# Smaller pieces for the first two images' inverse transforms, biases folded into the key and value weights, and a re-planned list schedule

## The chip, the cores and the metric

The kernel runs on one core of one Trainium2 chip. The metric is the device time of one execution in microseconds (us). Three runs of the kernel before gave 6176.5, 6177.5 and 6183.15 us; the median, 6177.5 us, is the time that counts. Engine names are those of the profile: PE is the matrix engine, PEld its weight loads, DVE the vector engine, ACT the scalar engine, POOL the GpSimd engine, SP the queue that starts most DMAs. A name with a q behind it (ACTq, PEq) is that engine's instruction queue when it issues or waits and computes nothing.

## The reference, cut to what matters

32 images of 128 channels and 64 x 64 pixels in float32 pass through two layers:

```python
x = x + conv(group_norm(x))            # butterfly transforms along w and h, a channel mix
                                       # per frequency, two inverse transforms, real part
t = to_tokens(x)                       # 4096 tokens of 128 channels for each image
n = layer_norm(t)
k = n @ Wk.T + bk                      # one 128 x 128 score matrix for each image:
v = n @ Wv.T + bv                      # its softmax replaces the sequence attention
t = t + n @ softmax(k.T @ v / sqrt(32)).T
n = layer_norm(t)
t = t + top2_gated_sum(n @ expert_w + expert_b, softmax(n @ router_w + router_b))   # 8 experts
x = from_tokens(t)
```

All eight experts are computed for each token, and the gates are zero for six of them.

## The kernel before, in words

The work has three stages, one after the other. **Stage 1** (to about 930 us) norms each image and takes it through the two forward transforms into `xf` in DRAM. **Stage 2** (to about 2550 us) goes through the 64 columns of frequencies: it builds the weights of a column (L610), mixes the channels of all images with them (L632) and stores the result to `pf` in DRAM (L651), eight stores for each half of the output channels. **Stage 3** (the rest) goes through the 32 images, one in about 109 us.

In stage 3 an image `b` passes through three functions, a slot apart, so that three images are in work at once:

- `conv(b)`: eight tiles `r0` to `r7` (two DMAs of 256 KB each, L825) come from `pf` by SP. `w_inverse(e)` (L838) multiplies one into a tile `pu` of two PSUM banks; there is a single such tile (pool `cps`, tag `cv`). `w_out` (L848) copies it to `u` on ACT, in four copies of 64 partitions by 512 elements. Then `h_inverse(g)` (L860) makes `py` from `u`, in the same two banks, and `h_out` (L868, DVE) adds it to the image `y` (one DMA of 2 MB, L819).
- `front(b)`: transposes to tokens (`pt` L919, copied by ACT L924), their moments on DVE (L893 to L906), a power on POOL (L911), normed tokens `xg` on ACT (L959), and their product with themselves `pg` (L970). `xg` has 129 columns, of which the last is one, so that `pg` also holds the sum over the tokens. From `pg` comes a chain of small steps on PE, DVE and ACT in turn: `gsum` (L983), `rows_mm` (`pa`: L987, L988, L989), `rows_out` (L994), `kv1` (`pb`: L998, L999), `kv1_out` (L1003), `kv2` (L1007, L1008), softmax (L1012 to L1027), `attn` (`pc`: L1031, L1032). L989, L999 and L1008 are products with one row, and bring in the two biases. Then `product` (`pp` L1058), `scaled` on ACT (L1071, L1075), `added` on DVE (L1086), second moments and gates.
- `experts(b)`: normed tokens (`xn` L1186), turned (`px` L1196, `xT` L1202), 64 products with the experts' weights (`pe` L1209, 128 x 512 each, three buffers of one bank, pool `eps`), each gated by DVE (`tm` L1220), summed by POOL (L1245, L1246, L1248), turned back (`po` L1255) and stored (L1261). In the last image DVE sums some pairs itself (L1232).

Every float32 product stands in the trace as two matmul records; a transpose is one.

The order on each engine is worked out when the kernel is built. `add(b, key, engine, us, at, run, after, take, free)` gives an operation its engine, an assumed duration `us`, a due time `at` in slots (moved by `SHIFT` for its kind of key), what it follows, and which buffers it takes and frees. `Plan.run` then plays the engines through with these durations: a free engine starts the earliest due operation whose predecessors and buffers are there. The order so found is issued as it is, and each engine works through its queue in that order, so that an operation that has to wait holds up what is queued behind it on its engine.

Ahead of the stage 3 plan stand its constants (L736 to L792): weights and biases by ACT's queue (L738 to L767), memsets on POOL (L753 to L762, L779), and a preparation that takes the experts' weights' mean out and adds their bias (`pm` L783, L784, L788; `pms` L791, L792). These are outside of the ordered block, and the trace shows them placed between its first instructions.

Of the kernel before, what the change touches and what calls it, by code (L numbers as in the profile page):

```python
# [90 lines left out]
def kernel(  # L91
# [57 lines left out]
    gmean = gmean.rearrange("p g r -> p (g r)")  # L149
    mhalf = cp.tile([P, NT], F32, name="mhalf")  # L150
# [7 lines left out]
    with ExitStack() as ph1:  # L158
# [274 lines left out]

        def butterfly(m, engine, eng, at, us):
# [76 lines left out]
        for s in range(B + 2):  # L511
# [23 lines left out]
            if s == 6:  # L535
                add("wr", "PE", 0.6, 6.0, weight_rows, [("b0", 5), "sel"], ("ps",))
                add("wd", "DVE", 0.8, 6.0, weight_matrices, ["wr"], (), ("ps",))
                butterfly(2, "POOL", nc.gpsimd, 7.0, 4.5)
                add("wo", "DVE", 1.2, 9.0, output_matrices, [("b2", 5)])
                add("wm", "SP", 0.5, 10.0, weight_taps, [("b2", 5)], (), (), 4.0)  # L540
            if 12 <= s < 16:
# [184 lines left out]

    cps = ctx.enter_context(tc.tile_pool(name="cps", bufs=1, space=PSUM))
    eps = ctx.enter_context(tc.tile_pool(name="eps", bufs=3, space=PSUM))
    tps = ctx.enter_context(tc.tile_pool(name="tps", bufs=3, space=PSUM))
    xp = ctx.enter_context(tc.tile_pool(name="xp", bufs=2))  # L730
    rp = ctx.enter_context(tc.tile_pool(name="rp", bufs=10))
# [5 lines left out]
    wk_sb = ct.tile([P, P], F32, name="wk_sb")  # L737
    nc.scalar.dma_start(wk_sb, wkT)  # L738
    wv_sb = ct.tile([P, P], F32, name="wv_sb")
    nc.scalar.dma_start(wv_sb, wvT)  # L740
    bk_sb = ct.tile([1, P], F32, name="bk_sb")
    nc.scalar.dma_start(bk_sb, bk.unsqueeze(0))
    bv_sb = ct.tile([1, P], F32, name="bv_sb")
    nc.scalar.dma_start(bv_sb, bv.unsqueeze(0))
    rb_sb = ct.tile([P, NE], F32, name="rb_sb")
    nc.scalar.dma_start(rb_sb, router_b.partition_broadcast(P))
    ew_sb = ct.tile([P, NE, P], F32, name="ew_sb")
    nc.scalar.dma_start(ew_sb, expert_w.rearrange("e d c -> d e c"))
# [5 lines left out]
    ntok = ct.tile([1, 1], F32, name="ntok")  # L754
    nc.gpsimd.memset(ntok, float(NPIX))
    ones = ct.tile([P, P], F32, name="ones")
    nc.gpsimd.memset(ones, 1.0)

    NG = 4
    xg = [ct.tile([P, 4, P + 1], F32, name=f"xg{i}") for i in range(NG)]  # L760
    for t in xg:
        nc.gpsimd.memset(t[:, :, P : P + 1], 1.0)  # L762
# [9 lines left out]
    with tc.tile_pool(name="prep", bufs=1) as prep:  # L772

        ebb = prep.tile([P, NE, P], F32, name="ebb")
        nc.scalar.dma_start(
            ebb.rearrange("p e c -> p (e c)"), expert_b.rearrange("e c -> (e c)").partition_broadcast(P)
        )
        om = prep.tile([P, P], F32, name="om")
        nc.gpsimd.memset(om, 1.0 / P)  # L779
# [9 lines left out]

        pe = eps.tile([P, 512], F32, tag="pe", name="pms")  # L790
        nc.tensor.matmul(pe[:, 0:NE], ones, prx[0][:, P + NE : QX], start=True, stop=True)  # L791
        nc.vector.tensor_copy(rws, pe[:, 0:NE])  # L792
# [5 lines left out]
        "ad": 0.75, "at": -0.21, "f": 0.63, "gt": 0.63, "h": -0.15, "ho": -1.5, "l": 0.63, "lg": 0.15,  # L798
        "m": -0.08, "na": -0.08, "pe": 0.49, "pg": -0.45, "pt": -0.03, "pwa": -0.08, "pwb": 0.15,
        "r": -0.33, "s": 0.1, "sa": 0.33, "so": -0.09, "st": 0.47, "to": 0.52, "va": -0.08, "vb": 0.15,  # L800
        "wo": 0.12, "x": 0.44, "xT": 0.44, "xg": 0.12, "xn": 0.35,
# [12 lines left out]
    xs, rs, tile_of = {}, {}, {}  # L814

    def transfers(b):
# [4 lines left out]
        def load_r(e):  # L821
            def run():
                t = rs[b, e] = rp.tile([P, 16 * n], F32, tag="r", name=f"r{b}_{e}")
                for r in range(2):
                    nc.sync.dma_start(t[r * n : (r + 1) * n], pfv[b, e, r])  # L825
            return run

        for e in range(8):
            add(b, f"r{e}", "SP", 0.2, b - 0.5 + 0.08 * e, load_r(e), take=("r",), late=5.0)
        add(b, "x", "SP", 0.1, b + 0.2, load_x, take=("x",), late=12.0)  # L830

    def conv(b):
# [39 lines left out]

        for e in range(8):
            at = b + 0.08 * e
            add(b, f"w{e}", "PE", 1.8, at, w_inverse(e), [f"r{e}"] + [(b - 1, f"h{k}") for k in range(4)], ("cv",), ("r",))
# [5 lines left out]
        for g in range(4):  # L881
            at = b + 0.68 + 0.07 * g
            add(b, f"h{g}", "PE", 2.15, at, h_inverse(g), [f"wo{e}_{oh}" for e in range(8) for oh in range(2)], ("cv",))
            add(b, f"ho{g}", "DVE", 1.25, at, h_out(g), [f"h{g}", "x"], (), ("cv",))

    def front(b):
# [8 lines left out]
        def moments(which):  # L895
# [3 lines left out]
            m2 = st.tile([P, 5, NT], F32, name=f"m2{which}_{b}", tag=f"m2{which}", bufs=2)  # L899
            total, diff, var, nmr, rstd = (m2[:, k, :] for k in range(5))  # L900
# [37 lines left out]
        for g in range(8):  # L938
            at = s1 + 0.016 * g
            add(b, f"pt{g}", "PE", 0.55, at, turn(g), [(b - 2, f"st{g}")] + [f"ho{k}" for k in range(4)], ("tl",))  # L940
# [5 lines left out]
        def nmr1():  # L946
            total, var, nmr, rstd = v[1]
            nc.vector.scalar_tensor_tensor(nmr, total, -0.5, rstd, ALU.mult, ALU.mult)

        add(b, "na", "DVE", 0.9, s1 + 0.14, nmr1, ["pwa"])  # L950

        def norm(g):
            def run():
                total, var, nmr, rstd = v[1]
                for k in range(4):
                    i = 4 * g + k
                    nc.scalar.activation(  # L959
                        xg[g % NG][:, k, 0:P], t[:, i, :], AF.Identity, bias=nmr[:, i : i + 1], scale=rstd[:, i : i + 1]  # L960
# [3 lines left out]
        def gram(g):  # L964
            def run():
                if g == 0:
                    v["pg"] = tps.tile([P, 512], F32, tag="tl", name=f"pg{b}")
                for k in range(4):
                    i = 4 * g + k
                    nc.tensor.matmul(  # L970
                        v["pg"][:, 0 : P + 1], xg[g % NG][:, k, 0:P], xg[g % NG][:, k, :],
# [4 lines left out]
        for g in range(8):  # L976
            at = s1 + 0.26 + 0.016 * g
            add(b, f"xg{g}", "ACT", 1.7, at, norm(g), ["na", (b if g >= NG else b - 1, f"pg{(g - NG) % 8}")], ("xg",))
            add(b, f"pg{g}", "PE", 1.06, at, gram(g), [f"xg{g}"] + ([f"pg{g - 1}"] if g else []), ("tl",) if g == 0 else (), ("xg",))
# [375 lines left out]
```

## Time and profile before

| | |
|---|---|
| median of three runs | 6177.5 us |
| the profiled execution's own time | 6179.07 us |
| its span, first to last instruction | 6177.3 us |
| stage 1, stage 2, stage 3 | about 930, 1620, 3625 us |
| from one image's L983 to the next, images 3 to 30 | 109.05 us |
| busy over the span: PE, POOL, DVE, ACT | 97%, 68%, 68%, 61% |
| granted PE clock, mean | 0.99 |

The page divides the span into 40 slices of 154 us and gives the busy share of each engine in tenths. Other views give the busy time in a stretch, a timeline by engine, who waited for whom, and all instructions of one line. A row of the timeline has the start, the time from the first start to the last end of a run of like instructions, the engine, the line, the tiles written and read, their shape and their number; behind it, in brackets, stands idle time before it and what ended that. PE's instructions overlap, so that what one costs in a full queue is the distance from its start to the next start, and not its duration.

### The profile page before, as it was taken

To read this page: it belongs to the slowest core of one execution; us is meant where nothing else is said; L and a number is where in the kernel's file an instruction comes from. 1 tells how busy PE (TensorE), PEld (TensorE's weight loads), DVE (VectorE), ACT (ScalarE), POOL (GpSimd) and SP (SyncE) were. 2 spreads that over 40 slices of the span, in tenths; PEclk is the share of its full clock that TensorE was granted. 3 is DMA by queue.
4 is the path that set the end of the run, shared out by engine and by line. 5 is a ranking of instruction groups with operands and counts; after the bars stand their busy time and mean duration, and the time that the engine had idled before them with its cause. 6 is when DMAs were issued, how large, how long until landed. Compare 5 with 4: busy or idle time off the path is not lost. (4 is left out here: it accounts for less than half of the span.)

```text
span 6177.3 us, 218388 instructions
## 1 busy us (share of the span) xinstructions
PE 5988.3 (97%) x94922; PEld 4714.0 (76%) x94922; DVE 4213.0 (68%) x7686; ACT 3759.2 (61%) x7089; POOL 4187.1 (68%) x3755
## 2 busy tenths in 40 slices
PE   7999999999999999789999999999999999999988
PEld 7999998999999999666666666666666666666654
DVE  5565545555555555358778787787878778787777
ACT  7666654555555555376666666766667666666753
POOL 2110006666666666238888888888888888888888
PEclk9999999999999999899999999999999999999999
DMA  6766666666666666622222222222212222131100
GB/s 201 236 227 232 233 213 170 173 172 171 174 172 172 172 172 172 160 74 95 69 84 78 65 96 64 88 76 71 91 62 94 67 86 78 64 96 64 67 21 26
DMA packets 556965, 756.55 MB, mean 122 GB/s; under 512 B 58466, under 2 KB 321892, under 8 KB 551908
## 3 DMA queue, kind: packets, MB, share of 16 engines
q1 hardware_dynamic: 554096, 741.38, 39.9%
q8 instruction: 745, 12.21, 0.9%
q14 instruction: 216, 1.77, 0.1%
q10 hardware_dynamic: 1908, 1.19, 0.1%
HBM read 406.80 MB, written 335.54 MB: 120 GB/s over the span
## 5 line engine op out<-in xcount | busy, mean ns | idle before, releaser
L1209 PE MATMUL pe<-ew_sb,xT 128*128 128x512 f32 x4096 | 1984.6, 601 | 44.8 <-DVE tm L1220 40.6
L1220 DVE TENSOR_TENSOR tm<-pe,oh 128x512 f32<-128x512 f32 x2028 | 1341.2, 684 | 535.0 <-PE pe L1209 422.4
L1245 POOL TENSOR_TENSOR tm<-tm 128x512 f32<-128x512 f32 x1014 | 1296.3, 1293 | 314.6 <-DVE tm L1220 263.4
L1209 PEld LDWEIGHTS pe<-ew_sb,xT 128*128 128x128 f32 x4096 | 691.0, 191 | 518.7 <-issue 333.1
L621 DVE COPY f<-g 128x1024 f32<-128x1024 f32 x512 | 627.2, 1225 | 665.7 <-PE g L610 665.7
L632 PE MATMUL m<-f,s 128*64 128x64 f32 x32768 | 1071.3, 224 | 5.0 <-POOL s L583 3.6
L632 PEld LDWEIGHTS m<-f,s 128*64 128x64 f32 x32768 | 1000.7, 138 | 66.8 <-POOL s L583 3.9
L583 POOL COPY s<-l 128x512 f32<-128x512 f32 x512 | 546.5, 1102 | 599.2 <-issue 518.7
L621 ACT COPY f<-g 128x1024 f32<-128x1024 f32 x512 | 518.5, 1013 | 576.9 <-PE g L610 550.3
L1248 POOL TENSOR_TENSOR tk<-tk,tm 128x256 f32<-128x256 f32 x1014 | 753.4, 743 | 79.5
L848 ACT COPY u<-pu 64x512 f32<-64x512 f32 x1024 | 594.1, 580 | 308.3 <-PE pu L838 285.0
L1246 POOL TENSOR_TENSOR tm<-tm 128x512 f32<-128x512 f32 x507 | 647.0, 1276 | 39.8
L838 PEld LDWEIGHTS pu<-qw,r 128*128 128x128 f32 x4096 | 503.6, 196 | 170.1 <-ACT u L848 92.2
L610 PE MATMUL g<-c,wst 9*128 9x128 f32 x16384 | 609.2, 284 | 4.6 <-ACT f L621 3.4
L838 PE MATMUL pu<-qw,r 128*128 128x128 f32 x4096 | 522.6, 282 | 63.3 <-ACT u L848 52.9
L610 PEld LDWEIGHTS g<-c,wst 9*128 9x128 f32 x16384 | 510.9, 187 | 40.6 <-ACT f L621 4.5
L344 POOL TENSOR_TENSOR grstd<-gms,mhalf 128x1 f32<-128x1 f32 x32 | 17.8, 555 | 735.6 <-DVE gms L340 735.6
L585 POOL TENSOR_SCALAR s<-l 128x512 f32<-128x512 f32 x256 | 509.5, 1990 | 0.0
L413 PE MATMUL pf<-ph,v 128*128 128x128 f32 x4096 | 491.4, 278 | 5.2 <-ACT z L378 1.1
L1261 ACT COPY so<-po 128x512 f32<-128x512 f32 x256 | 150.9, 590 | 563.0 <-issue 411.9
L893 DVE BATCH_NORM_STATS2 bs<-tk 128x6 f32<-128x128 f32 x2048 | 448.2, 279 | 56.3 <-ACT tk L924 44.2
L413 PEld LDWEIGHTS pf<-ph,v 128*128 128x128 f32 x4096 | 467.1, 192 | 15.1 <-ACT z L378 7.1
(166 smaller groups left out, 8499.9 us busy)
## 6 DMA issues: line engine op xcount, KB each, us to landing
xf<-f SPq DMA_DIRECT2D x512, 256.0 KB, 3.3
l<-xf SPq DMA_DIRECT2D x1024, 128.0 KB, 3.3
pf<-o SPq DMA_DIRECT2D x1024, 128.0 KB, 3.3
r<-pf SPq DMA_DIRECT2D x512, 256.0 KB, 4.8
x<-in_x_dram SPq DMA_DIRECT2D x256, 256.0 KB, 4.6
y<-in_x_dram SPq DMA_DIRECT2D x32, 2048.0 KB, 8.1
out_dram<-so SPq DMA_DIRECT2D x256, 256.0 KB, 2.1
tw<-in_tw_dram SPq DMA_DIRECT2D x6, 384.0 KB, 6.6
```

The source lines that it names most:

```text
L413: nc.tensor.matmul(pl[:, j * P : (j + 1) * P], vs[b][:, 8 * g + j, :], ph.rearrange("h r m -> h (r m)"), start=True, stop=True,)
L583: nc.gpsimd.tensor_copy(dst, src)
L610: nc.tensor.matmul(pg[g // 2][:, g % 2, m * P : (m + 1) * P], wst[rows, 16 * half + 4 * t + m, :], c[rows].rearrange("r h k -> r (h k)"), ...
L621: copy(f.rearrange("i m (g o) -> i m g o", g=2), tile_of["g", w, half, t][k].rearrange("i g (o m) -> i m g o", o=4))
L632: nc.tensor.matmul(ps[hh * n : (hh + 1) * n, q, :], s[:, h].rearrange("i k b -> i (k b)")[:, B * r : B * r + n], f[:, h, r, :], start=(r = ...
L838: nc.tensor.matmul(ps[:, k, :], rs[b, e][:, k * P : (k + 1) * P], qw.rearrange("w r m -> w (r m)"), start=True, stop=True,)
L848: nc.scalar.copy(u[r * n : (r + 1) * n, :, oh * n + 8 * e : oh * n + 8 * e + 8], ps[oh * n : (oh + 1) * n, :, r * n : (r + 1) * n].rearran ...
L1209: nc.tensor.matmul(ps, tile_of["xT", b, i // 4][:, i % 4, :], ew_sb[:, es, :].rearrange("d e c -> d (e c)"), start=True, stop=True,)
L1220: nc.vector.tensor_tensor(tile_of["tm", b, i // 2][:, i % 2, es, :], tile_of.pop(("pe", b, i, half)).rearrange("p (e c) -> p e c", c=P), t ...
L1245: nc.gpsimd.tensor_tensor(tm[:, k, 0:4, :], tm[:, k, 0:4, :], tm[:, k, 4:8, :], ALU.add)
L1246: nc.gpsimd.tensor_tensor(tm[:, :, 0:2, :], tm[:, :, 0:2, :], tm[:, :, 2:4, :], ALU.add)
L1248: nc.gpsimd.tensor_tensor(t[:, lo : lo + 2, :], t[:, lo : lo + 2, :], tm[:, :, m, :], ALU.add)
```

## The change

- **Biases in the weights.** `wk_sb`, `wv_sb`, `bk_sb`, `bv_sb` become one tile `wkv`. In the preparation the mean over the input channels is taken out of both weight matrices and a 128th of the bias added to every row (`pmk`, two DVE operations, as the experts' weights already had it). The first norm of `front` now gives the normed tokens plus one (bias `nmr + 1`, a new row `above`), and its row sum, 128 for each token, then brings the bias in. `xg` and `pg` have 128 columns. `rows_mm`, `rows_out` and the two row products of `kv1` and `kv2` are gone.
- **First two images.** For `b < 2` each `w_inverse` is split in two pieces of one bank, `w{e}_0` and `w{e}_1`, each of 32 smaller matmuls (two logical 64 x 64 results for each of 8 k), which use the three `pe` buffers. A piece is copied by one ACT copy of 128 partitions by 512 elements. `h_inverse` and `h_out` are split in two likewise. Other images are as before.
- **Loads.** The loads of `r0` and `r1` of image 0 are issued by POOL's queue and those of `r2` and `r3` by ACT's; they run ahead of the plan, behind the preparation. The other loads stay on SP.
- **Preparation.** `ew_sb`, `ebb` and `om` become constants that stage 1 loads on SP in four steps, in its slots 20 to 23. The preparation is moved into the ordered block, as its first part. `pms` uses `om` and a factor of 128 in place of a matrix of ones.
- **Order of pools.** `rp` (the tiles `r`) is opened before `xp`, so that it gets other memory, and `eps` before `cps`.
- **The schedule.** Assumed durations are changed (`w` 1.8 to 1.9, `h` 2.15 to 2.05, `pt`, `px`, `st` 0.55 to 0.48, `pg` 1.06 to 0.9, `pp` 0.3 m to 0.26 m, `pb` and `pb2` 0.7 to 0.35), and so is the table `SHIFT`. The order on all engines of stage 3 comes out of these anew.

```diff
+        def expert_load(k):
+            def run():
+                es = slice(2 * k, 2 * k + 2)
+                nc.sync.dma_start(ew_sb[:, es, :], expert_w[es].rearrange("e d c -> d e c"))
+                nc.sync.dma_start(
+                    ebb[:, es, :].rearrange("p e c -> p (e c)"), expert_b[es].rearrange("e c -> (e c)").partition_broadcast(P)
+                )
+            return run
...
+            if 20 <= s < 24:
+                add(("ew", s), "SP", 1.0, s, expert_load(s - 20), [("pf", s - 3, 4)], (), (), 4.0)
...
+    def prepare():
...
+        pe = eps.tile([P, 512], F32, tag="pe", name="pmk")
+        nc.tensor.matmul(pe[:, 0 : 2 * P], om, wkv.rearrange("d e c -> d (e c)"), start=True, stop=True)
+        nc.vector.scalar_tensor_tensor(
+            kvb.rearrange("p e c -> p (e c)"), kvb.rearrange("p e c -> p (e c)"), 1.0 / P, pe[:, 0 : 2 * P],
+            ALU.mult, ALU.subtract,
+        )
+        nc.vector.tensor_add(wkv, wkv, kvb)
...
-            return run
+                    queue.dma_start(t[r * n : (r + 1) * n], pfv[b, e, r])
+            return run
+
+        if b == 0:
+
+            first.extend(load_r(e, nc.gpsimd if e < 2 else nc.scalar) for e in range(4))
...
+        def w_inverse_piece(e, oh):
+
+            def run():
+                ps = tile_of["cw", b, e, oh] = eps.tile([P, 8, n], F32, tag="pe", name=f"pw{b}_{e}_{oh}")
+                for k in range(8):
+                    lo = (2 * k + oh) * n
+                    for r in range(2):
+                        nc.tensor.matmul(
+                            ps[r * n : (r + 1) * n, k, :], rs[b, e][:, lo : lo + n], qw[:, r, :], start=True, stop=True
+                        )
+            return run
+
+        def w_out_piece(e, oh):
+            def run():
+                nc.scalar.copy(
+                    u[:, :, oh * n + 8 * e : oh * n + 8 * e + 8],
+                    tile_of.pop(("cw", b, e, oh)).rearrange("h o w -> h w o"),
+                )
+            return run
...
-                        v["pg"][:, 0 : P + 1], xg[g % NG][:, k, 0:P], xg[g % NG][:, k, :],
+                        v["pg"][:, 0:P], xg[g % NG][:, k, :], xg[g % NG][:, k, :],
...
-            nc.tensor.matmul(pb[:, 0:P], v["gs"][:, 0:P], wv_sb, start=True, stop=False)
-            nc.tensor.matmul(pb[:, 0:P], v["rows"][:, 0:P], bv_sb, start=False, stop=True)
+            nc.tensor.matmul(pb[:, 0:P], v["gs"], wkv[:, 1, :], start=True, stop=True)
...
-            nc.tensor.matmul(pb[:, P : 2 * P], wk_sb, v["t1"], start=True, stop=False)
-            nc.tensor.matmul(pb[:, P : 2 * P], bk_sb, v["rows"][:, P : 2 * P], start=False, stop=True)
+            nc.tensor.matmul(pb[:, P : 2 * P], wkv[:, 0, :], v["t1"], start=True, stop=True)
...
-        add(b, "pa", "PE", 0.9, at, rows_mm, ["gs"], ("tl",))
-        add(b, "rows", "DVE", 0.42, at, rows_out, ["pa"], (), ("tl",))
-        add(b, "pb", "PE", 0.7, at, kv1, ["rows"], ("tl",))
+        add(b, "pb", "PE", 0.35, at, kv1, ["gs"], ("tl",))
...
     with tc.manual_schedule():
+        for run in first:
+            run()
         plan.run()
```

## Prediction

> **What bounds the kernel now.** I read the page's slices first, then the busy time of stage 3's even part, then who waits for whom on PE there, then its timeline over one image's chain, and last the timeline of the first 180 us of stage 3.
>
> ```profile
> PE   7999999999999999789999999999999999999988
> ...
> POOL 2110006666666666238888888888888888888888
> ```
>
> Each digit is 154 us. PE is at 90% or more from the second slice on, but for slices 17 and 18 (the start of stage 3, digits 7 and 8) and the last two. POOL, the next, is at 80 to 90%. The even part of stage 3:
>
> ```profile
> 3000.00:5924.00 2924.00, 2890.34 (x20229) 1952.29 (x20228) 2283.03 (x5066) 1944.15 (x4479) 2562.77 (x2200) 1.00 0.23 77
> ```
>
> The columns are the stretch, PE, PEld, DVE, ACT and POOL busy, the granted clock, the DMA share and GB/s. An image takes 109.05 us there, so POOL works 2562.77 / 2924 x 109.05 = 95.6 us for each and DVE 85.1; PE sets the pace, at full clock. Its waits, from 3100 to 5900 us:
>
> ```profile
> PE pe L1209 <- DVE tm L1220: 16.3, 26, 0.7
> PE pu L838 <- ACT u L848: 15.5, 52, 0.6
> ```
>
> Those 32 us (total, times, longest) over 25.7 images are 1.3 us an image, of 109.05. So what is taken off PE's queue there comes off the time, one for one, until POOL's 95.6 us are reached. One image's chain behind `pg`:
>
> ```profile
> 4071.34 1.02 PE L1209 MATMUL pe<-ew_sb,xT 128*128 128x512 f32 x2
> 4072.30 0.38 PE L987 MATMUL pa<-ident,gs 128*1 128x128 f32 x2
> 4072.51 0.38 PE L988 MATMUL pa<-wv_sb,gs 128*1 128x128 f32 x2
> 4072.83 0.38 PE L989 MATMUL pa<-bv_sb,ntok 1*1 1x128 f32 x2
> 4073.13 1.13 PE L1209 MATMUL pe<-ew_sb,xT 128*128 128x512 f32 x2
> 4074.09 0.38 PE L998 MATMUL pb<-wv_sb,gs 128*128 128x128 f32 x2
> 4074.41 0.48 PE L999 MATMUL pb<-bv_sb,rows 1*128 1x128 f32 x2
> 4074.82 1.13 PE L1209 MATMUL pe<-ew_sb,xT 128*128 128x512 f32 x2
> 4075.78 0.38 PE L1007 MATMUL pb<-t,wk_sb 128*128 128x128 f32 x2
> 4076.10 0.48 PE L1008 MATMUL pb<-rows,bk_sb 1*128 1x128 f32 x2
> 4076.51 3.70 PE L1209 MATMUL pe<-ew_sb,xT 128*128 128x512 f32 x8
> ```
>
> No idle stands between them, so a group costs the distance to the next start. The start of stage 3, as sums and in four of its instructions:
>
> ```profile
> 2548.30:2731.00 182.70, 121.55 (x1141) 106.05 (x1140) 59.55 (x180) 101.01 (x210) 18.05 (x22) 0.84 0.52 143
> ```
>
> ```profile
> 2555.86 3.75 PE L838 MATMUL pu<-qw,r 128*128 128x128 f32 x16 [7.53 <-issue]
> ...
> 2573.21 0.43 PE L791 MATMUL pms<-prx,ones 128*128 128x8 f32 x2
> ...
> 2576.86 3.40 PE L838 MATMUL pu<-qw,r 128*128 128x128 f32 x16 [2.48 <-ACT u L848]
> ...
> 2650.06 12.42 ACT L959 ACTIVATE xg<-tk,m 128x128 f32<-128x128 f32 x32
> ```
>
> PE is busy for 121.6 of 182.7 us at a clock of 0.84. Priced by the start distances of the even part (0.112 us a record of `pu`, 2.01 a `py` tile, 0.44 four transposes, 0.86 a `pe`), the work done there is 96 us. So 87 us are lost, and that caps what a quicker start can give.
>
> **Biases in the weights.** Gone from PE for each image: `pa`, 4073.13 - 4072.30 = 0.83 us; the row product in `pb`, 74.82 - 74.41 = 0.41; that in `pb2`, 76.51 - 76.10 = 0.41. The `pe` that followed `pa` took 0.96 to the next start where others take 0.86; that 0.1 goes too, if an ordinary pair follows. Together 1.65 to 1.75; I take 1.7. The 129th column of `pg` gives nothing: eight records take 0.89 us, 0.111 each, and those of `pu` with 128 columns 1.78 / 16 = 0.111. On DVE a copy of 0.41 us (`rows`) goes and an addition of 0.31 (as L1126) comes, which stands behind the power on the way to `xg`; PE has other images' work over it, and uncovered it is 0.3. Images 1 to 31 lie in the full part: 31 x 1.7 = **53 us**. PE stays the bound (107.4 against 95.6).
>
> **The new order.** Nothing in the trace shows it. Its gain is bounded by the idle left, 1.3 x 31 = 39 us. Its loss has the pairs of DVE as nearest rows: three `pe` buffers let PE run on for about 3 x 0.86 - 0.69 = 1.9 us without DVE, and one `added` group holds DVE for 0.55 + 3 x 0.28 = 1.4 us. Two in a row (2.8) would stop PE for 0.9; five such pairs in an image's eleven groups make 4.5 us, 140 us in all. I take 0: the assumed durations come nearer to the rows (`pt` 0.55 to 0.48, row 0.44; `pg` 1.06 to 0.9, row 0.89; `pp` 0.3 to 0.26, row 0.245), so a plan without waits is more nearly one on the chip too.
>
> **Image 0's transforms.** Now `pu` of `r0` starts at 2555.86 (landed), the rest waits: `r1`'s loads stand on SP behind eight stores to 2556.2, and `pm`, `pms` hold PE to 2573.5. The third tile starts at 2576.86, and the last `py` is added by 2623.4. After: the whole preparation is first in PE's queue, and it has a new wait, for `wkv` and `prx`. All of image 0's pieces are queued behind it, and ACT and DVE have nothing else to do, so the early `r0` to `r3` lie idle until then. Their memory seems to come free at 2559.5, when POOL's first memset of that pool ran (L753). ACT then needs 0.33 + 0.46 + 0.36 + 0.83 us to issue up to `prx` (its rows now; the 512 KB of `ew_sb` and 1.3 us of bias issues are ahead of it no more), and these landed 3.5 (`wk_sb`) to 7.8 us (`prx`) after issue: 2565 to 2569, I take 2567. Bounds: 2556, when `r0` lands now, if the memory is free sooner; 2574, when the preparation ends now. Then 16 pieces of 32 records, like half a `py` (64 in 2.01): 1.0 us each, or 1.9 at the pace of 3.75 for a `pu` that takes 2.05 in other places. With three buffers PE doesn't wait for ACT, whose copy takes 0.58; so 16 to 30 us, I take 20: 2587. `h`: 8 pieces of 1.0, a copy before and an addition of 0.7 behind, 10 to 12: **2598**. Gain 25 us, bounds 8 (2574, all slow) and 36 (2556; 2587 at best, as the last of `r` must land). `y` must be there by 2589: it is issued at 2577.25 now and lands 16 us later, 2593.7; with eight loads of 1.16 us gone from SP before it, about 2584.
>
> Two rules of the Trainium skill bear on this. By the page "DMA: Bandwidth & Descriptors", section "Issuing engines are not separate DMA queues", loads from SP, ACT and POOL share the same 16 engines, which speaks against the loads by other queues; the DMA share here was 0.89 from 2560 to 2576 us and 1.01 from 2576 to 2610, and by the rule those loads are worth only the 6.6 us that `r1` stood behind the stores, and not the 9 us that `y` gains above. By "TensorE: Matmul & The Clock Gate", section "What's actually happening", a busy window of about 3.4 us gives the full clock, and an idle one takes it away; the clock was 0.75 from 2576 to 2610 us with PE 54% busy, and by the rule the 16 pieces in a row would take about 18 us and not 20.
>
> **Image 0's tokens, beside image 1's transforms.** From `pt` (2623.46) to the first `pe` (2714.66) pass 91.2 us. `na` ends at 2643.25, but ACT's queue holds copies of `u` that wait for slow `pu`, so `xg` starts at 2650.06: 6.8 us. From `pa` to `pb` are 3.3 us, with a `pu` between; 3.0 go. The row products in `pb` and `pb2`: 0.8. `pc` waits behind another `pu` for 2.2. That is 12.8; ACT's copies of image 1 fall from 8 x 2.35 to 16 x 0.58, 9.5 us less, of which some shortens the 13 us of `pt`. I take **15 us**, bounds 3 (`pa` alone) and 25. With the former, 40 us of the 87, bounds 11 and 61.
>
> **Costed at nothing.** Eight DMAs more on SP in stage 1, at 0.45 us an issue 3.6 us in 110: there SP issues some 10 us of each 27.5, and `x` loads run ahead by two slots, with PE behind them 29.9 of 30 us busy; uncovered 3.6. `pmk` and two DVE operations (0.7 each, as L784): before the pieces, in the 2567. POOL's two loads have no row; ACT's issue took 0.2 to 1.0, and SP's 0.44, so below 4 us, with image 0's first POOL work at 2637. The end (from 6075 us on) keeps its work: 0, the new order within 5 either way.
>
> **Sum.** 53 + 25 + 15 = 93 us. The profiled execution took 6179.07 us; 6086, and the median lies 1.6 lower: **6085 us**, 1.5% less.
>
> **Rivals.**
> - *The preparation eats the start.* Pieces begin at 2574, and slowly; 5 us of the start remain: 6177.5 - 58 = 6119. For it: PE's queue is in order, and `prx` landed late. Against: less stands before it. 0.10.
> - *PE's saving is taken by waits.* DVE or ACT turns out to pace the images, the 109.05 stay: 6177.5 - 40 = 6137. For it: the evenness of 109.0. Against: 1.3 us of idle. 0.09.
> - *The new order also closes the gaps*, 30 of the 39 us: 6055; with more of the start, 6045. 0.09.
> - *Slower: pairs of `added` groups on DVE.* The new order puts two before a `tm`, five times in an image: 140 - 93 = 47 us more, 6225. It decides from 3 us an image, that is from 3.3 such pairs. For it: `ad` moves by half a slot in `SHIFT`. Against: the planner gives `pe` three buffers as well and counts 0.54 us for each of `ad`'s parts, a little more than the row's 0.46. 0.08.
> - *Nothing*, within 0.2% (12 us, about what a measurement of this kernel can tell from no change): half of this and half of that. 0.03.
>
> The forecast has 0.61. Its own range is 6060 to 6115 (start 11 to 61, order within 10). To leave out no more than 2 in 10, the range reaches to the waits' 6137 and the closed gaps' 6045: 6045 to 6138. Faster 0.61 + 0.10 + 0.09 + 0.09 = 0.89, same 0.03, slower 0.08.
>
> **What would show it.** The distance between two L983 falls from 109.05 to 107.4, with PE's waits near 1.3 us an image; above 108.5 the saving went into waits, and below 106.5 the order gave more. The first piece starts near 2567, the last addition of image 0 ends near 2598, the first `pe` stands near 2675. If the pieces start after 2573 or wait for `y`, or if `xg` again starts late after `na`, the start is wrong. If DVE's `tm` releases PE often, the last rival holds.

## The result, and the profile after

| | before | after |
|---|---|---|
| median of the timed runs (lowest to highest) | 6177.0 us (6176.0 to 6183.2) | 6112.0 us (6105.1 to 6114.5) |
| ratio, 95% interval | | 0.9891 (0.9874 to 0.9908) |
| span of the profiled execution | 6177.3 us | 6108.6 us |
| end of stage 2's last mixing product (L632 before, L648 after) to the first `pe` of image 3 | 499.6 us | 476.4 us |
| one image, first `pe` to first `pe`, mean of images 3 to 28 | 109.05 us | 107.68 us |
| first `pe` of image 29 to the end | 294.1 us | 288.0 us |

The gain is 65 us; 93 were forecast, 6085 us. The spans differ by 68.8 us, which the rows split: 23.2 at the start, 26 x 1.37 = 35.7 in images 3 to 28, 6.1 at the end, and 3.8 before stage 3. The last isn't the change's: over the profiles of this study stage 2 ends between 2541.9 and 2548.3 us in the three kernels with before's first stages, and between 2542.4 and 2547.4 in those with after's; before's own profile happens to be the latest.

The page's slices of after:

```profile
PE   7999999999999999889999999999999999999998
...
POOL 2110006666666666338888888888888888888888
```

PE's slices 17 and 18 read 8 and 8 where they read 7 and 8, and the last but one 9 where it read 8; otherwise PE is as full as before. The even part (stretch, PE, PEld, DVE, ACT, POOL, clock, DMA share, GB/s):

```profile
3000.00:5860.00 2860.00, 2792.28 (x19823) 1908.56 (x19822) 2289.91 (x5012) 1941.58 (x4429) 2531.78 (x2177) 1.00 0.25 77
```

PE is busy for 97.6% of it, against 98.8% before: work went, and idle time came. PE's waits in after from 3050 to 5836 us, with total, times and longest:

```profile
PE pe L1276 <- DVE tm L1287: 49.9, 52, 1.6
PE py L879 <- ACT u L867: 15.3, 24, 0.9
```

That is 2.5 us an image, twice the former 1.2, and one wait has grown: 1.9 us an image for `tm`, twice in each. The chain behind `pg`:

```profile
4034.29 1.02 PE L1276 MATMUL pe<-ew_sb,xT 128*128 128x512 f32 x2
4035.15 0.38 PE L1069 MATMUL pb<-wkv,gs 128*128 128x128 f32 x2
4035.37 1.88 PE L1276 MATMUL pe<-ew_sb,xT 128*128 128x512 f32 x4
4037.09 0.38 PE L1077 MATMUL pb<-t,wkv 128*128 128x128 f32 x2
4037.31 2.74 PE L1276 MATMUL pe<-ew_sb,xT 128*128 128x512 f32 x6
```

`pa` and the row products are gone, and each product that is left holds the queue for 0.22 us, where it held it for 0.32. The start, first as a sum and then in its instructions:

```profile
2544.50:2727.20 182.70, 138.24 (x2161) 120.71 (x2160) 69.02 (x207) 97.88 (x218) 30.55 (x25) 0.85 0.51 144
```

```profile
2542.95 1.29 POOL L836 DMA_DIRECT2D r<-pf  x2 [26.96 <-DMA pf<-o]
...
2550.02 1.00 ACT L658 COPY o<-m 64x1024 f32<-64x1024 f32 x1 [8.14 <-DMA pf<-o]
...
2566.61 1.19 PE L793 MATMUL pmk<-wkv,om 128*128 128x256 f32 x2 [20.13 <-DMA kvb<-in_bk_dram]
...
2571.24 9.13 PE L900 MATMUL pw<-qw,r 128*64 128x64 f32 x237 [1.30 <-DVE kvb L794]
...
2583.45 9.90 PE L900 MATMUL pw<-qw,r 128*64 128x64 f32 x242 [3.08 <-issue]
...
2598.16 9.81 PE L919 MATMUL pz<-hm,u 128*64 128x64 f32 x244 [3.52 <-issue]
...
2608.03 0.69 DVE L927 TENSOR_TENSOR y<-pz,y 128x512 f32<-128x512 f32 x1 [0.24 <-PE pz L919]
```

`pmk` waits 20 us for the biases, and the pieces wait behind it in PE's queue. Twice, after 2580 and 2594 us, PE then stands for over 3 us (3.3 and 3.7 from one start to the next) with no semaphore as the reason ("issue"). Image 0 is whole 64.1 us after the end of stage 2 (75.1 before).

### The profile page after: what moved, and what is told of

Read it like the earlier page. It is cut to its first block, busy times and chain, and to the rows that moved or that the text cites. A ratio compares the mean times of both kernels' runs of the same rounds, so it can differ in the third digit from the quotient of the medians.

```text
span 6108.6 us, 219213 instructions
## 1 busy us (share of the span) xinstructions
PE 5903.2 (97%) x95372; PEld 4682.8 (77%) x95372; DVE 4245.8 (70%) x7696; ACT 3762.1 (62%) x7057; POOL 4183.5 (68%) x3753
## 4 chain that ended last, share of the span: by engine, by line
PE 78%; DVE 9%; ACT 3%; DMA 2%; issue 2%; POOL 0%; SPq 0%; ACTq 0%; POOLq 0%; DVEq 0%
PE pe L1276 24%; PE m L648 17%; PE g L626 9%; PE pf L418 5%; PE pu L857 4%; PE pp L1125 4%; PE py L879 4%; PE pg L1052 4%; DVE tm L1287 2%; PE pv L396 2%; DMA out_dram<-so 2%; PE px L1263 2%; DVE eq L1200 1%; DVE eq L1199 1%; PE po L1322 1%
## 5 line engine op out<-in xcount | busy, mean ns | idle before, releaser
L1276 PE MATMUL pe<-ew_sb,xT 128*128 128x512 f32 x4096 | 1964.9, 601 | 80.1 <-DVE tm L1287 75.1
L1287 DVE TENSOR_TENSOR tm<-pe,oh 128x512 f32<-128x512 f32 x2028 | 1348.6, 685 | 360.8 <-PE pe L1276 339.6
L1312 POOL TENSOR_TENSOR tm<-tm 128x512 f32<-128x512 f32 x1014 | 1281.0, 1278 | 229.4 <-DVE tm L1287 205.7
L648 PE MATMUL m<-f,s 128*64 128x64 f32 x32768 | 1069.0, 224 | 4.8 <-POOL s L599 3.4
L648 PEld LDWEIGHTS m<-f,s 128*64 128x64 f32 x32768 | 998.4, 138 | 66.6 <-POOL s L599 3.7
L1315 POOL TENSOR_TENSOR tk<-tk,tm 128x256 f32<-128x256 f32 x1014 | 758.7, 748 | 79.5
L867 ACT COPY u<-pu 64x512 f32<-64x512 f32 x960 | 557.5, 581 | 223.7 <-PE pu L857 214.3
L1313 POOL TENSOR_TENSOR tm<-tm 128x512 f32<-128x512 f32 x507 | 651.5, 1285 | 39.8
L857 PEld LDWEIGHTS pu<-qw,r 128*128 128x128 f32 x3840 | 464.4, 193 | 93.3 <-issue 68.7
L1138 ACT ACTIVATE pp<-pp,m 128x128 f32<-128x128 f32 x1024 | 444.3, 434 | 136.7 <-PE pp L1125 110.8
L857 PE MATMUL pu<-qw,r 128*128 128x128 f32 x3840 | 471.7, 276 | 8.0 <-ACT u L867 8.0
L973 DVE BATCH_NORM_STATS2 bs<-tk 128x6 f32<-128x128 f32 x2048 | 453.1, 280 | 21.9 <-ACT tk L1006 7.0
```

The lines of the kernel that those rows point to most:

```text
L648: nc.tensor.matmul(ps[hh * n : (hh + 1) * n, q, :], s[:, h].rearrange("i k b -> i (k b)")[:, B * r : B * r + n], f[:, h, r, :], start=(r = ...
L857: nc.tensor.matmul(ps[:, k, :], rs[b, e][:, k * P : (k + 1) * P], qw.rearrange("w r m -> w (r m)"), start=True, stop=True,)
L867: nc.scalar.copy(u[r * n : (r + 1) * n, :, oh * n + 8 * e : oh * n + 8 * e + 8], ps[oh * n : (oh + 1) * n, :, r * n : (r + 1) * n].rearran ...
L1276: nc.tensor.matmul(ps, tile_of["xT", b, i // 4][:, i % 4, :], ew_sb[:, es, :].rearrange("d e c -> d (e c)"), start=True, stop=True,)
L1287: nc.vector.tensor_tensor(tile_of["tm", b, i // 2][:, i % 2, es, :], tile_of.pop(("pe", b, i, half)).rearrange("p (e c) -> p e c", c=P), t ...
L1312: nc.gpsimd.tensor_tensor(tm[:, k, 0:4, :], tm[:, k, 0:4, :], tm[:, k, 4:8, :], ALU.add)
```

## The experiments

Each kernel differs from after, unless before is named, by the edit shown. The times are medians, with the ratio to before and its interval; runs of one kernel mostly lie within 7 us of its median, and up to 12 (e4, whose profile is of its fastest run, 6235.3 us). Before was run again beside the experiments and had medians of 6177.0 to 6182.7 us, so the ratios compare better than the times, and a difference of a few us between two kernels shows nothing. "Period" is the time from one first `pe` to the next, in the profiled execution, and PE's waits are given for one such period (means of images 3 to 28).

**The pace of the images: biases and order apart.** Before with the bias edits alone, and before with the new order alone:

```diff
 e4_bias_only (before)
+ pmk; above; xg and pg of 128 columns; kv1 and kv2 of one product; pb, pb2 0.35; na 1.2
- rows_mm, rows_out, the two row products
 e9_order_only (before)
+ SHIFT of after; w 1.9, h 2.05, pt, px, st 0.48, pg 0.9, pp 0.26 m
```

> The kernel before, with nothing but the biases folded into the key and value weights (no rows_mm, rows_out, row products; 128 columns; the two assumed durations of pb and pb2 0.35, na 1.2); loads, pieces, preparation's place, SHIFT and other durations as before. By the prediction the period falls by 1.7 to 107.35 and the time by 53 us: 6124, with 2 us more at the start for the added constants. By the ledger of the two traces what PE has to do falls by 1.84 us an image, and if the waits stay at 1.25 the period is 107.2: 6121. Rival (the saving is taken by waits on DVE in any order): waits rise above 2 us, period 108.2 or more, 6150 or more.

> The kernel before, with the new table SHIFT and the new assumed durations of w, h, pt, px, st, pg and pp, and nothing else; the bias products stay. With e4 (biases alone, period 111.6) this makes the square: before 109.05, both 107.68. Theory (saving and order interact: only the order made for the shorter queue has few waits): waits 2 us or more, period 109.5 to 112, 6190 to 6270. Rival (the order is better by itself, and gains whatever the biases do): waits of 1.5 us or less, and, with the 0.8 us less that the new order's ledger shows at unchanged products, period 108.3 or less, 6155 or less.

| period, us (PE's waits in it) | order of before's table | of after's table |
|---|---|---|
| biases as before | 109.05 (1.22) | e9: 114.31 (5.35) |
| biases in the weights | e4: 111.62 (4.54) | 107.68 (2.53) |

e4 took 6246.9 us, 1.0101 (1.0086 to 1.0116); e9 took 6346.2, 1.0273 (1.0257 to 1.0288). Each half alone makes the kernel slower, and both together make it faster: the two are not terms of a sum. (The last cell is the whole change; that its other edits, at the start, leave the period alone is taken from the runs below, where they move it by 0.2 us at most.) The bias edit takes 1.84 us an image off PE in e4 as in after. But the planner makes a new order for what is left, and in e4 PE waits in it, here in one of its stops:

```profile
4032.84 4.48 PE L1199 MATMUL pe<-ew_sb,xT 128*128 128x512 f32 x6 [2.06 <-DVE tm L1210]
```

The six records that follow the wait take 4.48 us, where six take 2.74 in after's chain above: behind many such waits the clock was at half, 61 us in 17 windows between 3050 and 5800 us. There was none of that in before or after. The waits of e9 in the same stretch:

```profile
PE pu L839 <- ACT u L849: 78.9, 33, 2.4
PE pe L1210 <- DVE tm L1221: 21.1, 21, 2.1
```

Here it is ACT's copies for the single `pu` tile that PE waits for. The same for after with before's table:

```diff
 e3_old_shift
- SHIFT = "ad": 0.16 ... "ho": -0.67 ... "pg": -0.08 ... "xn": 0.64
+ SHIFT = "ad": 0.75 ... "ho": -1.5 ... "pg": -0.45 ... "xn": 0.35
```

> The changed kernel with the table SHIFT of the kernel before; durations and everything else stay. In the changed kernel an image takes 107.68 us, of which PE waits 2.53 (1.25 before); once in each image PE waits 1.55 us for DVE, which works 6.7 us without a product of gates there. Theory (the new order put a statistics group, 0.86 us, between the second logits and the first maximum): with the old table that wait falls to about 0.6 us, the waits to 1.3 us, the period to 106.4, 26 x 1.3 = 34 us over the even part, though the start may lose some. Rival (with a shorter PE queue DVE's long stretch binds in any order): waits stay at 2.3 us or more and the period at 107.5 or more.

6270.2 us, 1.0143 (1.0128 to 1.0158); period 112.9, waits 5.51, 72 us at half clock in 21 windows. So none of the three mixed kernels had an order with as few waits as before or after. No run took the products away and held before's order.

**The same order, more work.** Products that nothing reads, added inside operations that the plan already has:

```diff
 e12_more_kv
+            for k in range(5):   # kv1; three such in kv2
+                nc.tensor.matmul(pb[:, lo : lo + P], v["gs"], wkv[:, 1, :], start=True, stop=True)
```

> The changed kernel, with eight more products in kv1 and kv2 (five and three, of the same size as the ones there, into columns of pb that nothing reads), at the same planned durations, so that all orders stay. They put 8 x 0.22 = 1.76 us on PE in each image, about what the folded biases took off. Theory (in a fixed order PE's work counts one for one in the even part, and the misses of e4 and e9 came from their orders): the period rises by 1.6 to 1.9, to 109.3 to 109.7, 46 to 55 us in all. Rival (waits take up the slack, so that the biases' saving was worth little in this order too): the period rises by less than 0.9.

6166.3 us, 0.9981 (0.9972 to 0.9990). The period is 109.63, where the six kernels below that differ from after only in the start have 107.85 to 107.89: 1.74 to 1.78 us more for 1.79 us of products, from start to start. Against after's own profile, 107.68, it is 1.95; after has the six kernels' work, but waits 2.53 us, most of the difference at `u`, where they wait 2.70 to 2.75. So with the order held fast, PE's work does count about one for one, as the prediction's first step had it, and its waits stay at 2.70.

**The wait for `tm`.** Once in an image DVE does this in after (start, duration, operation):

```profile
3974.44 0.68 DVE L1287 TENSOR_TENSOR tm<-pe,oh 128x512 f32<-128x512 f32 x1
3975.04 1.08 DVE L1205 TENSOR_TENSOR lg<-lg,m 128x256 f32<-128x256 f32 x1
3976.15 0.84 DVE L1206 TENSOR_TENSOR lg<-lg,rb_sb 128x256 f32<-128x256 f32 x1
3976.91 0.86 DVE L973 BATCH_NORM_STATS2 bs<-tk 128x6 f32<-128x128 f32 x4
3977.69 0.40 DVE L1198 TENSOR_REDUCE tops<-lg 128x32 f32<-128x256 f32 x1
...
3979.12 1.38 DVE L1200 TENSOR_TENSOR eq<-eq,rank 128x256 f32<-128x256 f32 x1
...
3980.99 0.92 DVE L1202 TENSOR_TENSOR oh<-eq,tops 128x256 f32<-128x256 f32 x1
3981.84 0.68 DVE L1287 TENSOR_TENSOR tm<-pe,oh 128x512 f32<-128x512 f32 x1
3982.57 1.13 PE L1276 MATMUL pe<-ew_sb,xT 128*128 128x512 f32 x2 [1.55 <-DVE tm L1287]
```

From 3975.04 to 3981.84 there is no `tm`: two additions to the logits, a statistics group, and the choice of the first expert, L1198 to L1202, 4.1 us long and planned with 2.6. PE fills its three `pe` buffers, does a `pu` and some transposes, and stops for 1.55 us. In before, at the same place, a `tm` stood between the additions and the choice:

```profile
4012.50 1.38 DVE L1139 TENSOR_TENSOR lg<-lg,rb_sb 128x256 f32<-128x256 f32 x1
...
4013.81 0.68 DVE L1220 TENSOR_TENSOR tm<-pe,oh 128x512 f32<-128x512 f32 x1
4014.41 0.40 DVE L1131 TENSOR_REDUCE tops<-lg 128x32 f32<-128x256 f32 x1
...
4017.53 1.88 DVE L1220 TENSOR_TENSOR tm<-pe,oh 128x512 f32<-128x512 f32 x3
```

At this place the longest stretch without one was 3.1 us. To test it, the stretch was made shorter in after's order, and, in another kernel, open to the planner. The first, e10, leaves out the tie-break of the first choice (three DVE operations, which matter where two logits are equal), so it is a probe and not a replacement:

```diff
 e10_no_tie
             nc.vector.tensor_reduce(m, v["lg"], AX.X, ALU.max)
+            if k == 0:
+                nc.vector.tensor_tensor(oh, v["lg"], by_expert(m), ALU.is_equal)
+                return
 e7_split_max
-        add(b, "f1", "DVE", 2.6, ...)
+        add(b, "f10", "DVE", 1.4, ...); add(b, "f11", "DVE", 1.8, ...); add(b, "f12", "DVE", 0.9, ...)
```

> The changed kernel, with the tie-break of the first choice of expert left out (three of the five DVE instructions, L1200 to L1202 of the changed kernel, 2.7 us; the equality is written as the choice itself), at the same planned durations, so that all orders stay as they are. Theory (PE's wait of 1.55 us in each image is the tail of DVE's 6.7 us without a product of gates): at 4.0 us the three buffers cover nearly all, the wait for DVE falls from 1.9 to about 0.5 us an image, and the period by 1.4 to 106.3 to 106.5: about 6072. Rival (the images are paced by something else, and the wait reappears at another place): the period falls by less than 0.5.

> The changed kernel, with each first maximum of the gates (five DVE instructions, 4.1 us, planned at 2.6 as one operation) planned as three operations of 1.4, 1.8 and 0.9 us, so that products of gates can stand between. Instructions and data are the same, only their order changes. Theory (PE's one wait of 1.55 us in each image comes from DVE's 6.7 us without such a product, more than the three buffers cover): the wait falls under 0.5 us, the waits of an image from 2.5 to 1.3 us, the period from 107.7 to 106.5, and the kernel to about 6080. Rival (any new order brings waits elsewhere): the period is 107.7 or more, 6112 or more.

e10 took 6057.7 us, 0.9805 (0.9788 to 0.9821). Its waits:

```profile
PE pe L1279 <- DVE tm L1290: 24.2, 28, 0.9
PE py L879 <- ACT u L867: 0.6, 2, 0.5
```

Nothing is changed on PE, and 2.8 us less on DVE in this one place (the stretch is now 4.0 us) take 1.6 to 1.8 us off the period (106.07). The wait of 1.55 us is gone, so it came from this stretch; with it go the other that after has in each image, 0.37 us at the second choice just behind, and the wait for `u`, some 0.6 to 0.8 us an image in the kernels with the full choice. What is left is a wait that after hardly has, at another long stretch of DVE, the gates of the chosen experts (5.5 us without a `tm`):

```profile
3976.95 1.13 PE L1279 MATMUL pe<-ew_sb,xT 128*128 128x512 f32 x2 [0.92 <-DVE tm L1290]
```

e7 took 6373.4 us, 1.0318 (1.0301 to 1.0335), with a period of 116.38:

```profile
PE pu L857 <- ACT u L867: 130.3, 61, 2.7
PE pg L1052 <- ACT xg L1041: 17.8, 10, 1.8
```

The wait at which it was aimed fell, to 0.15 us an image. But the new order puts `pu` tiles next to each other, and most wait 2.4 us for the copies of the one before. Here durations nearer to the rows did not make an order nearer to one without waits.

**The start: loads.** The early `r` by one queue, and back on SP:

```diff
 e1_all_pool
-first.extend(load_r(e, nc.gpsimd if e < 2 else nc.scalar) for e in range(4))
+first.extend(load_r(e, nc.gpsimd) for e in range(4))
 e2_loads_on_sp
-            first.extend(load_r(e, nc.gpsimd if e < 2 else nc.scalar) for e in range(4))
-            early = b == 0 and e < 4
+            early = False
```

> The changed kernel, with all four early loads of image 0 on POOL's queue and none on ACT's. Theory (the loads on ACT hold the last copy of stage 2): in the changed kernel ACT's last copy of L658 ran at 2550.02 us, 5.2 us after the last L648 ended, because two loads that wait for stores stood ahead of it in ACT's queue; without them it runs within 1.1 us, the last stores, the constants' loads and the first piece (L900) come 4 to 5 us earlier after the end of L648 (19 us in place of 23.4), and the kernel gains 3 to 5 us: 6107 to 6109. Rival (the loads and their bandwidth set the start): the copy runs early, but the first piece and the last addition of image 0 stay within 1 us after the end of L648, and the time stays at 6112.

> The changed kernel, with the early loads of image 0 put back on SP, in the plan. The early loads lie unused until the preparation has run (r0 landed at 2549.1 us, the first piece began at 2568.0). Theory (they are worth nothing, and hold ACT): the last copy runs at once, the constants come 4 to 5 us earlier, the last r tile 2 to 4 us later because SP issues eight loads more; the time is 6108 to 6114, within 4 us of the changed kernel. Rival (the early loads are what makes the start quick): the r tiles bind, image 0 ends 8 us or more later, 6120 or more.

6113.0 us, 0.9889 (0.9874 to 0.9904), and 6113.5, 0.9890 (0.9873 to 0.9906): in this kernel the loads by other queues bring nothing. In after's rows above, ACT's last copy of stage 2 starts at 2550.02, though PE's last `m` is done at 2544.6, since the loads ahead of it in ACT's queue wait for stores. In e1 and e2 that copy waits for nothing, and the first piece starts 19.5 and 17.2 us after stage 2, where after's starts at 23.4. In e1 none of it is left at image 0's end, which comes after 64.9 us (64.1 in after): PE waits 3.6 us for `kvb` and stands more often. In e2's profile, of the fastest of its four runs, image 0 is whole after 58.8 us, yet the median is after's. These runs can't show what early loads are worth to pieces that are free to start, for here the preparation holds the pieces until 2567.96, and the last of `r0` to `r3` had landed at 2557.2 us.

**The start: pieces and preparation.**

```diff
 e5_no_pieces
-        if b < 2:
+        if b < 0:
 e6_late_prep
+    def prepare_late():        # pmk, pms and what follows them
...
+                if b == 0 and e == 7 and oh == 1:
+                    prepare_late()
 e11_late_prep_pool = e6_late_prep + e1_all_pool
```

> The changed kernel, with the first two images' transforms in whole two-bank tiles, as the other images' are (the pieces undone, all else kept). The prediction gave pieces, loads and preparation together 40 us of the start. Theory (the single two-bank tile makes PE and ACT take turns: 2.0 to 3.8 us of products and 2.4 us of copies for each of 8, then 2.1 and 1.2 for each of 4): image 0's last addition comes about 14 us later (78 us after the end of L648 in place of 64.1), image 1's as much again, the start to image 3 takes 495 to 505 us in place of 476, and the kernel 6130 to 6145. Rival (PE's stands for instructions give the pieces' gain away, and larger matmuls, a quarter as many, don't have them): within 8 us of the changed kernel.

> The changed kernel, with the second half of the preparation (pmk and pms, which wait for wkv and prx) put behind all but the last of image 0's w pieces on PE. The prediction said that the preparation holds the pieces while r0 to r3 lie idle. Theory (it holds them): the first piece runs 5 us after the end of L648 in place of 23.4 us, and image 0's last addition comes 8 to 12 us earlier (52 to 56 us after it in place of 64.1), bound by r7 and y (landed 31 and 41 us after it); the start to image 3 takes 468 us in place of 476. Rival (PE then stands for its instructions while loads fill the DMA engines, as it did in the changed kernel twice for 3.3 and 3.7 us without waiting for a semaphore): pieces begin early, but such stands grow to 12 us or more, and the last addition moves by less than 4 us.

> The changed kernel, with the late preparation of e6 and the early loads on POOL as in e1: what the runs so far point to as the quickest start. Theory (with the pieces free to begin, ACT's held copy, which delays the stores by 5 us and with them r4 to r7 and y, now counts): image 0's last addition comes 2 to 4 us before that of e6 (45 to 47 us after the end of L648 in place of 48.5), the start to image 3 takes 460 to 462 us, the kernel 6100 to 6103. Rival (PE stands for its instructions again, as in e1, and takes it back): 464 us or more, 6104 or more.

e5 took 6138.2 us, 0.9935 (0.9921 to 0.9950), with image 0 whole after 83.6 us: the pieces are worth 26 us by the medians and 23 by the start in its profile (499.4 us to image 3, against 476.4). e6 took 6104.0, 0.9881 (0.9866 to 0.9896), and e11 6103.3, 0.9879 (0.9865 to 0.9894). In e6 PE does this:

```profile
2549.66 9.61 PE L904 MATMUL pw<-qw,r 128*64 128x64 f32 x256 [2.63 <-issue]
2565.31 3.68 PE L904 MATMUL pw<-qw,r 128*64 128x64 f32 x64 [6.04 <-DMA r<-pf]
2572.32 7.14 PE L904 MATMUL pw<-qw,r 128*64 128x64 f32 x160 [3.33 <-DMA r<-pf]
```

The pieces start 4.6 us after stage 2 and not 23.4, so the early tiles are there in time; now it is `r4` to `r7` that are waited for. Image 0 is whole after 48.5 us, 15.7 sooner, and 12.4 of that reach image 3 (464.0 us). The medians differ by 8, and their intervals overlap; e6's period of 107.87, against 107.68 in after's profile, takes 5 back over 26 images. In e11 image 0 is whole after 45.2 us and image 3 starts after 462.6; its total can't be told from e6's.

**The stands without a semaphore.** Of PE's stands in the pieces, the theory was that instructions come late beside the loads of image 1; so those were postponed:

```diff
 e8_late_image1
+            if b == 1:
+                add(b, f"r{e}", "ACT", 0.9, ..., load_r(e, nc.scalar), [(0, "wo7_1")], take=("r",), late=5.0)
```

> The changed kernel, with the loads of image 1 (r and y, 6 MB) issued by ACT behind image 0's last w copy, in place of SP beside image 0's pieces. Theory (PE's stands of 3.3 and 3.7 us in image 0, without a semaphore, are waits for instructions whose loads queue behind those 6 MB): the second, in the h pieces, shrinks below 1 us, and the first below 2; image 0's last addition comes 4 to 7 us earlier, though image 1 comes later and the time may be up to 20 us longer. Rival (the stands belong to the many small matmuls themselves, 240 pairs a refill): both stay at 3 us or more.

6118.0 us, 0.9902 (0.9888 to 0.9917). The second stand shrank from 3.7 to 0.8 us, and image 0 was whole after 53.8 us, 10 sooner; but the first stayed at 3.0, and new ones came in image 1's pieces, beside the postponed loads:

```profile
2582.12 7.28 PE L906 MATMUL pw<-qw,r 128*64 128x64 f32 x242 [2.80 <-issue]
2594.98 3.60 PE L925 MATMUL pz<-hm,u 128*64 128x64 f32 x116 [0.55 <-issue]
2602.01 1.34 PE L906 MATMUL pw<-qw,r 128*64 128x64 f32 x21 [3.08 <-issue]
2618.01 5.50 PE L906 MATMUL pw<-qw,r 128*64 128x64 f32 x127 [2.27 <-issue]
```

In this run such stands went where the loads went. What the queues show in after from 2578 to 2584 us:

```profile
q1 hardware_dynamic: 174, 2.24, 98.7%
q8 instruction: 1, 0.02, 1.1%
```

The 16 engines are full with data, and one packet of 16 KB of instructions starts at 2580.85 us, 0.7 after PE's last matmul. Another starts at 2595.55, 1.1 after its next stop. Over the ten profiles with pieces, up to 2640 us, PE has 29 stands of over 2 us without a semaphore (a kernel's first piece left out), and at 28 of them such a packet starts between 0.3 us before PE's stop and 2.0 after it. But the two at 2571.47 and 2587.27 go with no such stand, the 29th, of 4.6 us in e11, has no packet, and the first stand of e8 has loads of `r4` to `r7` and `y` beside it still. That PE waited for instructions fits these rows; it is not shown, and no run took the loads away altogether. The Trainium skill, "Runtime: NRT & Kernel Launch", section "Instruction fetch mechanics", has instructions coming in blocks of 16 KiB, with a cost that is mostly hidden. The size agrees with the packets; if the stands are waits for blocks, then the cost was not hidden in these 40 us.

## Why the prediction was right or wrong

- **The total** lay within the stated range, and in part by luck. The period was to be 107.4 us with waits near 1.3 (the rows give 1.24) and is 107.68, with waits of 2.53, where before had 1.22: 1.31 us of waits that the prediction did not count met 0.84 of saved work that it did not count either.
- **Biases, 53 us: the mechanism held, the size did not.** PE lost 1.84 us of work an image (`pa` 0.83, two row products of 0.41, and 0.19 at `pb`), a little more than the 1.7 taken, and e12 shows that such work counts in full while the order stays. The step that failed is "what is taken off PE's queue there comes off the time, one for one": the order did not stay, and PE's waits rose by 1.31. With another 0.84 of work saved by the order (less for `pe`, `px` and `pu`), 1.37 is left, 42 us for 31 images. The rival "PE's saving is taken by waits" held by half: of 2.68 us less work in an image, waits took 1.31.
- **"The new order: 0" failed as a step of its own.** The square has -1.37 for both, +2.57 and +5.26 for each alone. A term for the order that can be added to one for the biases does not exist here.
- **The last rival** had the right engine, tile and kind of row, DVE without a `tm`, and the wrong place. It asked for pairs of `added`, 2.8 us long; what stops PE is the choice of the first expert behind two additions and a statistics group, 6.8 us, in a row that the timeline of before had already in two parts.
- **Image 0, 25 us: 11 measured**, near the lower bound of 8. The first piece was forecast at 2567 and started at 2567.96, for the reason given, the constants' late loads. But stage 2 ended 3.8 us earlier in this profile, so the piece came 23.4 us behind it and not 18.7, and 4.7 of the gain were lost there. The prediction had nothing for ACT's queue, in which loads that wait for stores hold the last copy; without these, in e1, the first piece comes after 19.5. The pieces took 25.4 us to 2593.4, and not 20, and `h` with its additions 15 and not 11. In them stand the two stops of 3.3 and 3.7 us, and 1.3 for `kvb`, which the prediction had counted as done before the first piece. The clock was 0.76 and 0.70 in the two long runs of pieces, 9.1 and 9.7 us: 2.2 and 2.9 us lost. The prediction's other estimate for the pieces, 18 us, counted on PE staying busy, and PE did not.
- **"The preparation eats the start"** was the rival with the true mechanism. e6 prices it: 15.7 us of image 0, 12.4 of the start to image 3, and some 8 of the total, which is not clear of the scatter.
- **Loads by other queues, 9 us at `y` and 6.6 at `r1`: nothing.** `y` landed at 2593.0 us in after, 48.4 behind stage 2, where it was 49.3 in before (at 2597.6; the prediction's 2593.7 is the issue plus 16 us, but its second half took 19), with a DMA share of 1.01 to 1.03 in the two long runs of pieces; and the early `r` lay idle behind the preparation.
- **Tokens, 15 us: about 10.** The start gained 23.2; less 11 for image 0 and 2.7 for two periods' saving, 9.6 are left. The mark was wrong, though: the first `pe` was forecast near 2675 and stood at 2704.9. The new order does the tokens of image 1 between: its `gsum` comes at 2702 us, at 2756 before.
- **Costed at nothing:** the loads in stage 1 cost nothing that shows (the last of `pf` there at 929.4 and 930.0 us). POOL's issue of a load, which had no row, took 0.5 to 0.8 us. The end gained 6.1, 3.4 more than two periods.

By steps, against 93: the biases gave 12 less (41 over the 30 periods in these rows), image 0 14 less, the tokens 5 less, the end 3 more, and 4 came from stage 2's scatter: 69, the difference of the spans.

## What to carry to other kernels

Where a planner makes the order, work that is removed buys only what the order made anew leaves of it: measure the edit with its new order, and each alone, before adding up gains. A saving on the engine that is full can be eaten by the longest stretch in which the engine that frees its buffers does something else (6.8 us here, and when it was cut to 4.0, another of 5.5); read such stretches in the timeline, and don't go by the average of that engine's load. Of loads that are moved earlier, ask what stands ahead of their reader in its own queue.

## What the runs showed of the hardware

One DVE operation, the same code in both kernels, has three prices. Its line in before, and in after (shortest, median and longest ns):

```profile
L1133 DVE TENSOR_TENSOR eq<-eq,rank x64: 424/835/1386, 2705.3 to 6091.7; 128x256 f32<-128x256 f32 x64
```

```profile
L1200 DVE TENSOR_TENSOR eq<-eq,rank x64: 424/1378/1390, 2696.9 to 6022.8; 128x256 f32<-128x256 f32 x64
```

In after it took 424 to 426 ns in the three instances with POOL idle beside it. POOL was busy for 90% or more of the other 61, and there the price goes with what POOL does. Beside its additions of 512 elements (L1312, L1313, 1.27 us each) 60 took 1.37 to 1.39 us, and beside one of 256 (L1315, 0.73) one took 0.83, so each some 0.1 us more than the operation beside it. Before has 34 of its 64 beside the shorter addition, at 0.83 to 0.84 us, and 28 beside the longer, at 1.37 to 1.39: the order decides which POOL operation stands there, and so the median. L1287, which reads PSUM and SBUF, stayed at 666 to 694 ns in all its instances, and L973, with one input, at 268 to 297. The Trainium skill, "SBUF — State Buffer", section "Who interferes with whom", says that a DVE operation with two inputs in SBUF contends with GpSimd operations that read SBUF, and one with a single SBUF input does not; these rows agree. Three operations of the choice of an expert are of this kind (0.96, 1.38 and 0.92 us in the stretch shown, where each takes 0.42 with POOL idle), which accounts for the 4.1 us where the plan has 2.6.

In the full part, from 3050 to 5800 us, half clock was seen in the four kernels with long PE waits: e3, e4, e7 and e9, with 72, 61, 195 and 61 us of it, most of its windows behind a wait of 1.8 to 3.1 us as in the row shown. Not every such wait was followed by one: several of 2.0 to 2.5 us were not. There was none in before, after and the other kernels, whose longest PE waits there are 0.7 us (before) and up to 1.6.
